# A two-layer decoder: a causal-attention batch stops counting as open from its first output product on

## The chip, the cores and the metric

The kernel runs on one core of one Trainium2 chip. The metric is the device time of one execution in microseconds (us), the median of several runs. Five engines work side by side: TensorE (in the profile PE for its matmuls and PEld for its weight loads), VectorE (DVE), ScalarE (ACT), GpSimd (POOL) and SyncE (SP), which here only issues data transfers (DMAs). Matmul results land in PSUM, in eight banks of 128 x 512 float32; everything else is held in SBUF.

## The reference

The input is four batches of 512 tokens by 512 features. Two layers follow, each with a self attention, a cross attention and a feed-forward part; after each of the six parts the result is added to its input and normalized over the features. The part that the change touches is the self attention of layer 1:

```python
kqv = x @ Wqkv + bqkv
kqv = kqv.reshape(b, s, 3, NUM_HEADS, HEAD_SIZE)        # 16 heads of 32
scores = jnp.einsum('bsnh,btnh->bnst', k, q) / math.sqrt(HEAD_SIZE)
scores = jnp.triu(scores) + -10000.0 * jnp.tril(ones, k=-1)
attn = jax.nn.softmax(scores, axis=2)
out = jnp.einsum('bnkq,bknh->bqnh', attn, v)
return out.reshape(b, s, NUM_HEADS * HEAD_SIZE) @ Wo + bo
...
x = _layernorm(x + _L1_attn_ref(x, L1_attn_Wqkv, L1_attn_bqkv, L1_attn_Wo, L1_attn_bo), axis=-1)
x = _layernorm(x + _L1_xattn_ref(x, ctx_2048, mask_BxS2_bk0), axis=-1)
x = _layernorm(x + _L1_ffn_ref(x, L1_ffn_gate_up_packed, L1_ffn_gate_up_scales, L1_ffn_down_packed, L1_ffn_down_scales), axis=-1)
```

The cross attention of layer 1 scores each token against its batch's 512 context rows, and the last feed-forward part works with 4-bit weights.

## The kernel before, in words

The six parts are called A to F, and a part with a batch is a task: D2 is the layer 1 self attention of batch 2, E0 the layer 1 cross attention of batch 0. Each task is a Python generator that emits instructions and yields at the end of a turn. `lanes` (line 1254) goes through the tasks in the order A0 to A3, B0 to B3, and so on to F3 (line 38). It keeps at most two tasks open; each round it lets every open task emit one turn, so the instructions of the two are interleaved. A new task opens when fewer than two are open, when the part before it is done for its batch, and when the task that was opened last has said `"next"` (lines 1263 to 1270). A task that has ended is taken off the list (lines 1273 to 1275).

The order in which turns are emitted isn't the order in which engines work. It is a priority: the compiler takes for each engine the earliest emitted instruction that is ready and finds a free tile, so a transfer or a transpose whose inputs are there can be moved far forward. Tiles come from shared pools: 69 of 2 KB a partition for operands (`op`), 13 for short-lived results (`tp`), 12 for the batches' x (`xp`, line 27), 4 for weights on their way, and the eight PSUM banks.

A self-attention task (`l1_attn`, line 820) loads its four x tiles, 128 tokens each, and then goes through these turns:

- three turns without work, then four with the 16 transposes of x (tile dx, line 828); its results are split into a high and a low half (dxh, dxl);
- the projections of the first four heads' keys and queries (dq, `project`, line 832) and the values (dv, line 872). A product of two such pairs is three matmuls (`mm3`, line 149). `stack` (line 848) copies the halves of each head into one tile (stk) by twelve DMAs a projection, on the queues of SP and POOL;
- 16 turns with one head each (line 961): scores (ds, line 908), maximum and mask on DVE (de, line 919), exponential on ACT (de, line 923), transposes (dT, line 933), copies (dpT, line 942), and for four heads at a time the product with the values (do, line 953). The further projections stand in the turns of heads 0, 1, 4, 5, 8 and 9. At head 7 (`D_NEXT`, line 968) the task says `"next"`;
- the drain of what is still queued, four transposes back to token order (dto, line 990), the merging with the sums of the masked part (line 981), four transposes to feature order (dF, line 996);
- four turns with the output products (dy, line 1007), each followed one turn later by the addition to x and its statistics (line 1001);
- the normalization (`finish`, line 229): four more turns, at whose end the x tiles are stored (line 238).

The bias of the output is added to x ahead of that, on POOL (line 994). Work that belongs to no batch is emitted beside certain tasks (`BESIDE`, line 40): beside D1 to D3 the 4-bit codes of the last part are unpacked on DVE (`l1_ffn_codes`, line 1061; lines 1074, 1075 and 1082), a block every third turn; beside E2 they are loaded back, with the rest of the last part's weights (`l1_ffn_weights`, line 1093).

The cross attention E (`l1_xattn`, line 1015) loads x, mask and context, transposes x (ex), computes scores (es, line 1048) and a softmax (lines 1041, 1042), transposes the weights (ep) and multiplies by the context (pv).

Of the kernel before, what the change touches and what calls it, by code (L numbers as in the profile page):

```python
# [68 lines left out]
class Net:  # L69
# [750 lines left out]
    def l1_attn(self, b):  # L820
# [183 lines left out]
        for i in range(NT):  # L1004
            pipe.tick()
            ps = self.pa("dy")
            self.mm3(ps, [(self.cols(oF[k], slice(i * P, (i + 1) * P)), self.w1[k, 3]) for k in range(NT)])
            pipe.later(1, add, ps, i)
            yield
        yield from pipe.drain()  # L1010
        self.finish(pipe, x, ln, 3, b)
        yield from pipe.drain()
# [241 lines left out]
def lanes(order, task, step):  # L1254

    todo = [(e.strip("+!"), e[0] == "+", max(1, e.count("!"))) for e in order]
    plain = [name for name, _, _ in todo]
    live, done = {}, set()  # L1260
    n, said = 0, 9
    while todo or live:
        if todo and len(live) < 2:
            name, soon, times = todo[0]
            before = chr(ord(name[0]) - 1) + name[1]
            if (before in done or before not in plain) and (said >= times or not live or soon):
                todo.pop(0)
                live[name] = task(name)
                last = name
                n, said = n + 1, 0  # L1270
        for name, g in list(live.items()):
            word = next(g, "end")
            if word == "end":
                live.pop(name)
                done.add(name)
            elif word == "next" and name == last:
                said += 1
        step(n)


def body(tc, args, phases=range(6)):
    with ExitStack() as ctx:
        net = Net(ctx, tc, args)
        net.gamma = net.load(net.c("gamma", [P, 1]), args["gamma"].to_broadcast([P, 1]))
        if 0 in phases:
            net.l0_attn_weights()
        net.bg = {("B", 0): net.l0_xattn_ctx(0), "C0": net.l0_ffn_scales(), "C": net.l0_ffn_weights(), "D": net.l1_attn_weights(), "F0": net.l1_ffn_codes(), "F": net.l1_ffn_weights()}
        f = [net.l0_attn, net.l0_xattn, net.l0_ffn, net.l1_attn, net.l1_xattn, net.l1_ffn]
        plain = ORDER.replace("+", "").replace("!", "").split()
        order = ORDER.split() if len(phases) == 6 else ["ABCDEF"[p] + str(b) for p in phases for b in range(B)]  # L1290

        def step(n):
            if len(phases) == 6:
                for first, last, key in BESIDE:
                    if plain.index(first) < n <= plain.index(last) + 1:
                        next(net.bg[key], None)

        def start(name):
            return f["ABCDEF".index(name[0])](int(name[1]))

        lanes(order, start, step)
# [68 lines left out]
```

## Time and profile before

| what | value |
|---|---|
| median of 3 runs | 1580.65 us |
| lowest and highest | 1579.52 and 1584.71 us |
| profiled execution, its own time | 1581.65 us |
| its span, first to last instruction | 1580.0 us |
| mean granted TensorE clock | 0.996 |
| PE busy | 1515.4 us |
| DVE, ACT, POOL busy | 1232.9, 1021.3, 666.2 us |

The profiled execution's time is 1.65 us above its span. Where things lie in it, by the views of the tiles: the transposes of x begin at 745.9 us for D0, 819.1 for D1, 941.2 for D2 and 1020.5 for D3; the first heads at 776.1, 859.3, 974.6 and 1061.5; the first output products at 903.4, 957.9, 1102.5 and 1158.1. The cross attention's transposes begin at 1141.2 (E0), 1181.7 (E1), 1194.7 (E2) and 1237.8 (E3). The first product of the last part (fg) begins around 1256 us.

A busy time is the union of an engine's instructions. A row of the view by stretches has the stretch, its length, and for each engine busy time and number of instructions, then the granted TensorE clock and the transfers' share and rate. A row of the order of time has start, length, engine, line, operation and tiles, and in brackets the engine's idle time before it with what ended it. A row of the waits has who waited, for whom, the total in us, how many times and the longest.

### The profile page before, as it was taken

Reading aid. Unit: us, or ns where it says so; the run is one execution under the profiler, and the core shown is the slowest. Engines: PE = TensorE matmul, PEld = TensorE weight load, DVE = VectorE, ACT = ScalarE, POOL = GpSimd, SP = SyncE. Lnnn points to the kernel's source line nnn. Section 1 sums busy time; section 2 is a strip of 40 time slices with the busy share of each in tenths; the row PEclk is TensorE's granted clock in tenths of the full one; section 3 lists DMA queues with packets and bytes.
Section 4 is the critical chain, followed back from the end, with each engine's and each line's share of the span. In section 5 each row is a group of like instructions: output and inputs, shape, how many; then the busy total and the mean of one; then the engine's idle time right before and its main releaser. Section 6 shows DMA issues by size and latency. Waiting matters only on the chain.

```text
span 1580.0 us, 25595 instructions
## 1 busy us (share of the span) xinstructions
PE 1515.4 (96%) x8222; PEld 1090.1 (69%) x8222; DVE 1232.9 (78%) x2658; ACT 1021.3 (65%) x2208; POOL 666.2 (42%) x672
## 2 busy tenths in 40 slices
PE   8999999999999999899999999999999999999996
PEld 6888786444544674477777668777687777777875
DVE  6486589999976688777577797767786888888896
ACT  5333336988878877888696864969634445545554
POOL 6673663555535303430435323353225344344342
PEclk9999999999999999999999999999999999999998
DMA  7043344455214744653434445633436630020101
GB/s 255 29 157 124 113 154 132 149 173 176 78 48 123 224 137 133 201 185 134 134 102 118 104 141 148 171 97 92 125 123 222 233 110 12 24 81 1 54 1 53
DMA packets 134150, 192.31 MB, mean 122 GB/s; under 512 B 17265, under 2 KB 52081, under 8 KB 134017
## 3 DMA queue, kind: packets, MB, share of 16 engines
q1 hardware_dynamic: 129888, 182.23, 36.3%
q0 software_dynamic: 4128, 8.46, 2.2%
q8 instruction: 65, 1.06, 0.3%
q14 instruction: 69, 0.56, 0.1%
HBM read 117.75 MB, written 47.71 MB: 105 GB/s over the span
## 4 chain that ended last, share of the span: by engine, by line
PE 63%; DVE 17%; ACT 8%; issue 6%; DMA 3%; POOL 3%; SPq 0%; ACTq 0%; DVEq 0%; POOLq 0%
PE fg L1185 7%; PE facc L1168 5%; PE dT L933 3%; DVE fg L1141 3%; PE pg L687 3%; PE had L755 2%; PE dn L741 2%; DVE bsm L474 2%; PE pu L689 2%; ACT de L923 2%; PE bo L498 2%; PE do L953 2%; PE qk L156 2%; PE qk L155 2%; PE qk L154 2%
## 5 line engine op out<-in xcount | busy, mean ns | idle before, releaser
L1141 DVE SCALAR_TENSOR_TENSOR fg<-fg,gs,fg 128x512 f32<-128x512 f32 x220 | 163.2, 745 | 30.9 <-ACT fg L1133 15.3
L923 ACT ACTIVATE de<-de,dm 128x128 f32<-128x128 f32 (+3 forms) x256 | 142.9, 563 | 11.3 <-DVE dm L919 10.9
L1185 PE MATMUL fg<-fxh,gu 128*128 128x512 f32 x352 | 140.2, 398 | 6.1 <-DVE fg L1141 3.1
L919 DVE CUSTOM_DVE_ANT_0 de<-ds,negm,thr 128x128 f32<-128x128 f32 (+3 forms) x256 | 126.4, 546 | 19.4 <-PE ds L908 16.0
L482 POOL TENSOR_SCALAR be<-be,bsm 128x512 f32<-128x512 f32 x128 | 96.5, 766 | 103.8 <-DVE bsm L480 72.7
L1185 PE MATMUL fg<-fxl,gu 128*128 128x512 f32 x352 | 137.4, 390 | 0.1
L664 POOL TENSOR_TENSOR hl<-g,hh 128x512 fp32r<-128x512 f32 x64 | 83.4, 1309 | 110.2 <-ACT hh L663 90.2
L1145 POOL TENSOR_TENSOR fg<-fg,fg 128x512 f32<-128x512 f32 x44 | 60.2, 1367 | 139.6 <-DVE fg L1141 60.0
L476 ACT ACTIVATE be<-bs,bsm 128x512 f32<-128x512 f32 x128 | 87.3, 690 | 31.1 <-DVE bsm L474 29.2
L845 POOL TENSOR_TENSOR dql<-dqf,dqh 128x512 fp32r<-128x512 f32 x32 | 41.4, 1295 | 150.8 <-ACT dqh L844 150.6
L933 PE MATMUL dT<-ident,de 128*128 128x128 f32 x640 | 92.0, 280 | 8.5 <-ACT de L923 6.4
L933 PEld LDWEIGHTS dT<-ident,de 128*128 128x128 f32 x640 | 72.3, 142 | 28.3 <-ACT de L923 14.0
L1185 PEld LDWEIGHTS fg<-fxh,gu 128*128 128x128 f32 x352 | 66.0, 188 | 30.1 <-DVE fg L1141 12.7
L474 DVE TENSOR_REDUCE bsm<-bs 128x1 f32<-128x512 f32 x128 | 83.4, 672 | 0.0
L498 PE MATMUL bo<-bpT,cT 128*64 128x512 f32 x256 | 76.7, 618 | 2.4 <-ACT bpT L489 1.2
L248 PEld LDWEIGHTS bT<-ident,be 128*128 128x128 f32 x512 | 54.9, 141 | 34.0 <-issue 11.5
L248 PE MATMUL bT<-ident,be 128*128 128x128 f32 x512 | 73.2, 281 | 3.6 <-POOL be L482 2.1
L1185 PEld LDWEIGHTS fg<-fxl,gu 128*128 128x128 f32 x352 | 66.1, 188 | 12.8 <-DVE fxl L146 0.4
L352 POOL TENSOR_TENSOR z<-z,rope_cos 128x512 f32<-128x512 f32 x32 | 46.8, 1473 | 64.8 <-DVE zs L349 57.8
L1133 ACT ACTIVATE fg<-fg,gs 128x512 f32<-128x512 f32 x88 | 60.1, 684 | 20.6 <-PE fg L1185 20.4
L687 PE MATMUL pg<-qT,tb 128*128 128x512 bf16 x256 | 66.8, 381 | 4.5 <-ACT qT L649 2.8
L1159 POOL TENSOR_TENSOR fhl<-fg,fhh 128x512 fp32r<-128x512 f32 x44 | 58.5, 1331 | 29.5 <-ACT fhh L1158 29.3
(355 smaller groups left out, 4640.3 us busy)
## 6 DMA issues: line engine op xcount, KB each, us to landing
x<-x SPq DMA_DIRECT2D x176, 256.0 KB, 3.0
had_scratch<-hw SPq DMA_DIRECT2D x64, 256.0 KB, 2.3
z<-had_scratch SPq DMA_DIRECT2D x64, 256.0 KB, 5.8
stk<-dqh SPq DMA_DIRECT2D x192, 64.0 KB, 2.1
tw<-in_wg_t SPq DMA_DIRECT2D x32, 256.0 KB, 3.8
tw<-in_wu_t SPq DMA_DIRECT2D x32, 256.0 KB, 3.7
tw<-in_wd_t SPq DMA_DIRECT2D x32, 256.0 KB, 2.8
p<-in_gu_p SPq DMA_DIRECT2D x22, 256.0 KB, 3.1
```

What stands on the lines that cost most here:

```text
L248: self.nc.tensor.transpose(pt[:, i * P : (i + 1) * P], srcs[i][:, j * P : (j + 1) * P], self.ident)
L474: nc.vector.tensor_reduce(sm[:, h : h + 1], ps, AX.X, ALU.max, negate=True)
L476: nc.scalar.activation(e, ps, AF.Exp, bias=sm[:, h : h + 1], accum_out=sm[:, 2 + h : 3 + h])
L482: nc.gpsimd.tensor_scalar(es[h][i], es[h][i], sm[:, 4 + h : 5 + h], 1.0, ALU.mult, ALU.mult)
L498: nc.tensor.matmul(po[0][h * 64 : h * 64 + 64, :], cT[j][:, c : c + 64], pTs[h], start=j == 0, stop=j == NT - 1)
L664: nc.gpsimd.tensor_tensor(lo, g, hi.bitcast(F32), ALU.subtract)
L687: nc.tensor.matmul(pg, tern["wg_t"][k, c][:, m], qT[k], start=k == 0, stop=k == NT - 1)
L919: nc.vector.tensor_tensor_reduce(es[i], ps, self.negm[:, 384 - P * i :], -1.0, self.thr[:, i : i + 1], ALU.add, ALU.min, n4[:, i : i + 1])
L923: nc.scalar.activation(es[i], es[i], AF.Exp, bias=n4[:, i : i + 1], scale=-1.0, accum_out=den[:, hh * 4 + i : hh * 4 + i + 1])
L933: nc.tensor.transpose(pt[:, o + (i - j) * P : o + (i - j + 1) * P], es[i][:, j * P : (j + 1) * P], self.ident)
L1141: self.emitted["DVE"] = nc.vector.scalar_tensor_tensor(y[u], ps, s, y[u], ALU.mult, ALU.add)
L1185: nc.tensor.matmul(ps, self.gu[i, u][:, g * P : (g + 1) * P], xT[g][n], start=n == 0, stop=n == 1)
```

## The change

At its first output product (i = 0) the attention task now yields the word `"tail"`. `lanes` notes the names that have said it, and no longer counts such a task among the open ones when it decides whether another may begin. The task itself goes on as before, one turn a round, until it ends. Only task D says `"tail"`; the other conditions for opening a task are the same. So while an attention batch is in its last nine turns, a third task may be open.

```diff
@@ -1006,7 +1006,7 @@
             ps = self.pa("dy")
             self.mm3(ps, [(self.cols(oF[k], slice(i * P, (i + 1) * P)), self.w1[k, 3]) for k in range(NT)])
             pipe.later(1, add, ps, i)
-            yield
+            yield "tail" if i == 0 else None
         yield from pipe.drain()
         self.finish(pipe, x, ln, 3, b)
         yield from pipe.drain()
@@ -1257,10 +1257,10 @@
 
     todo = [(e.strip("+!"), e[0] == "+", max(1, e.count("!"))) for e in order]
     plain = [name for name, _, _ in todo]
-    live, done = {}, set()
+    live, done, tails = {}, set(), set()
     n, said = 0, 9
     while todo or live:
-        if todo and len(live) < 2:
+        if todo and len(live.keys() - tails) < 2:
             name, soon, times = todo[0]
             before = chr(ord(name[0]) - 1) + name[1]
             if (before in done or before not in plain) and (said >= times or not live or soon):
@@ -1275,6 +1275,8 @@
                 done.add(name)
             elif word == "next" and name == last:
                 said += 1
+            elif word == "tail":
+                tails.add(name)
         step(n)
```

## The prediction

> **What bounds the kernel now.** I read four things in this order: the page, for the busiest engine; stretches of the span, for where that engine idles; the waits and the order of time in those stretches; and last the DMA queue, for whether loads are late.
>
> ```profile
> span 1580.0 us, 25595 instructions
> PE 1515.4 (96%) x8222; PEld 1090.1 (69%) x8222; DVE 1232.9 (78%) x2658; ACT 1021.3 (65%) x2208; POOL 666.2 (42%) x672
> ```
>
> TensorE (PE) is busy 96% of the span. The change doesn't alter a single piece of arithmetic, so it can only move PE's 64.6 us of idle time. Everything up to the first output product of attention batch D0 keeps its place; that product starts at 903.2 us (the view of the tile dy). So only idle time after 903 us is in play.
>
> Busy time by stretch; PE is the third number:
>
> ```profile
> core 0: us, PE busy (x) PEld busy (x) DVE busy (x) ACT busy (x) POOL busy (x), PEclk, DMA share, GB/s
> 850.00:900.00 50.00, 46.21 (x275) 35.75 (x273) 34.59 (x98) 36.91 (x98) 14.35 (x23) 1.00 0.46 125
> 900.00:950.00 50.00, 47.30 (x326) 34.15 (x325) 46.27 (x123) 32.33 (x92) 17.56 (x20) 1.00 0.42 133
> 950.00:1000.00 50.00, 49.89 (x252) 39.73 (x254) 37.41 (x97) 31.37 (x79) 16.91 (x26) 1.00 0.55 160
> 1050.00:1100.00 50.00, 48.62 (x289) 38.40 (x289) 34.65 (x99) 38.65 (x102) 17.10 (x26) 1.00 0.39 102
> 1100.00:1150.00 50.00, 47.03 (x317) 34.00 (x317) 38.82 (x106) 32.89 (x93) 16.79 (x20) 0.97 0.45 137
> 903.00:1180.00 277.00, 267.43 (x1665) 204.46 (x1664) 215.19 (x573) 186.10 (x501) 97.27 (x125) 0.99 0.43 125
> 1180.00:1260.00 80.00, 74.15 (x366) 58.29 (x364) 60.24 (x123) 38.12 (x83) 35.01 (x27) 1.00 0.69 240
> ```
>
> From 903 to 1180 us PE idles 277 - 267.43 = 9.6 us, and in the cross attention behind it (1180 to 1260) 80 - 74.15 = 5.9 us. All that this change could fill is therefore 15.5 us, 1% of the span. It isn't spread evenly: 2.70 us idle in 900:950 and 2.97 in 1100:1150, where D1 and D3 end their heads, but 0.11 in 950:1000, where D2 begins its heads with D1 nearly done.
>
> The order of time on PE at the end of D1's heads, and PE's waits from 903 to 1250 us (total, times, longest):
>
> ```profile
> 931.18 0.55 PE L933 MATMUL dT<-ident,de 128*128 128x128 f32 x3 [0.64 <-ACT de L923]
> 933.39 0.44 PE L933 MATMUL dT<-ident,de 128*128 128x128 f32 x2 [0.74 <-ACT de L923]
> 941.22 1.91 PE L248 MATMUL dx<-ident,x 128*128 128x128 f32 x16
> ```
>
> ```profile
> PE dT L933 <- ACT de L923: 4.7, 10, 0.7
> PE es L154 <- DVE exl L146: 1.5, 2, 1.3
> ```
>
> PE waits for ScalarE's exponentials, and D2's transposes (dx) stand ten microseconds behind these holes. Are they late because D2's input is late? The DMA queue says no:
>
> ```profile
> 769.10 2.02 SPq L238 DMA_DIRECT2D x<-x  x4
> 771.41 2.63 SPq L252 DMA_DIRECT2D x<-x  x4
> 1175.11 2.72 SPq L238 DMA_DIRECT2D x<-x  x4
> 1178.42 2.16 SPq L252 DMA_DIRECT2D x<-x  x4
> ```
>
> Each burst of four loads (L252) follows a burst of four stores (L238). The x pool has twelve tiles, three batches of four, so a load waits for the store of the batch three before it. D0's transposes began at 745.9 us, before the burst issued at 741.4 had all landed (747.2), so that burst was D1's and the one at 771.41 is D2's, behind C3's stores. D2's input was landed at 776.8 us, 164 us before its first transpose. The burst at 1178.42 is likewise E2's, behind D3's stores.
>
> **The change part by part.** No instruction is added or removed. By the generators, an attention batch takes 55 turns and its end is seen on the 56th: transposes on turns 4 to 7, first projections on 9 and 10, values on 11 to 14, heads on 15 to 30, output products on 47 to 50. Openings, counted from D0's: before D1 22, D2 56, D3 78, E0 112, E1 134, E2 143; after D1 22, D2 47, D3 69, E0 94, E1 116, E2 125. D2 comes 9 turns earlier, and E0 and all behind it 18. A turn saved isn't time saved: the PE work of the dropped turns stands in others.
>
> *Loads.* Four x loads per batch move forward on SP's queue. They have no value for D2, as shown. They are moved past D0's four stores; those wait for VectorE, not for SP, and the loads take 0.3 to 0.5 us each to issue. Zero; the cover is the 164 us.
>
> *The hole at the end of a batch's heads.* With D2's transposes (16, 1.91 us) and projections put before D1's drain, they can fill 2.70 us, and E0's can fill the 2.97 us beside D3. Bounds: 0 and -5.7. The third batch's own casts (dxh, 0.59 us each) join the ScalarE queue that PE is waiting for here, so I take half, -2.8. POOL's bias additions for D2 (four at L994) move from 942.9 into its gap from 906.7 to 935.0: nothing.
>
> By the Trainium skill (Perfetto Trace Analysis, Identifying the Most-Contended Engine) matmul occupancy is a poor measure of headroom and weight-load busy share is the better one. PE's weight loads are busy 11.39 us of 920:940 and 10.93 of 1120:1140 against a mean of 14.69 in twelve stretches of 20 us there; by that rule about 20 x 3.3/14.69 + 20 x 3.76/14.69, some 9.6 us, could be had, an estimate, and the sum would be 4 us below mine. I stay with the idle time, since this trace has the narrow value products (do) in just these stretches, whose loads take 0.11 us each against the usual 0.19.
>
> *The start of D2's heads.* Before, D2's heads start at 974.6 us beside the last of D1, idle 0.11. After, the distance D1 to D2 is 25 turns, so they start beside D1's merges and output transposes, just as D1's heads stood beside D0's (22 turns; 850:900, idle 3.79) and D3's beside D2's (1050:1100, idle 1.38). Bounds: +1.3 and +3.7; I take the mean of the two, (3.79 + 1.38)/2 - 0.11 = +2.5.
>
> *E2's input.* This is a new wait. E2 opened 10 turns after D3's end; now it is 1 turn. Its x tiles are D3's. From D3's last output product (1169.2) through add, statistics, normalization, store and load to E2's landed tiles (1184.7) took 15.5 us. Work that PE surely has behind that product is E1's 16 transposes at 0.11 and 48 score products at 0.227, 12.6 us. What is left is 2.9 us. Queued behind the load on SP are E1's and E2's context loads. Bounds: 0 (the compiler's order finds other PE work, such as E0's last products) and 15.5 (none is left over). I take +2.9.
>
> *Background steps.* The code unpacking beside D1 to D3 needs some 70 turns and had 90; it now gets 72. It ends about where E0 opens and stays covered by heads: zero. Uncovered, the rest would be pumped where the last layer first asks for it: per block 0.65 + 0.52 + 0.55 us of VectorE, so two blocks left over cost 3.4 us.
>
> Sum: -2.8 + 2.5 + 2.9 = +2.6 us. The profiled execution took 1581.65 us, 1.65 more than its span and 1.0 above the median 1580.65. Against the median this makes 1583.2.
>
> **The rivals.**
>
> *A, the forecast: holes move.* Two are half filled and two open. Own range -2 to +8 us.
>
> *B, the third batch really fills.* PE takes D2's and E0's work in every hole, and D2's head start finds D3's projections as cover. For it: 950:1000 shows that PE can run at 99.8% with this mixture of work, and ScalarE has room (32.33 of 50). Against it: the trace also has 46.21 of 50 in a stretch with two open batches. Half of the 15.5 us goes, 8 us: 1572.6.
>
> *C, slower: the 69 shared tiles.* The attention's weights and bias hold 33, which leaves 36, and one batch alone needs up to 36 of them around its seventh head (counted over its turns in the code). Head stacks (stk) already wait on SP for tiles that other heads still read:
>
> ```profile
> SPq L853 <- ACT dpT L942: 19.5, 7, 7.6
> SPq L853 <- PE do L953: 12.2, 4, 10.8
> ```
>
> PE hardly notices today: D0's second stack landed at 790.6 us and head 4 began at 792.6, 2.0 us later. It decides once a stack is more than these 2 us later than now. With D1, D2 and D3 crowded alike, one longest wait of 7.6 less 2.0 at each of three later stacks of D2 is 16.8 us; 1581.65 + 16.8 - 1.0 = 1597.4. Against it: the pair D0 and D1 has the same crowding at 22 turns and lost only 3.79 us in its worst stretch. The Trainium skill (Perfetto Trace Analysis, Optimization Strategy) says that a recurring gap on the engine that should be saturated can mean too little buffer space for the next tile; that speaks against a third batch on unchanged pools, and it would make the sum that of this rival.
>
> *D, nothing moves.* The compiler already hoists what is ready (D2's loads), so an earlier place would leave the same order: 1580.65. Against it: D2's transposes were ready for 164 us and weren't hoisted.
>
> **How the numbers follow.** A 0.50 (0.02 faster, 0.28 same, 0.20 slower, as its range reaches past the bound of 4.7 us mostly upwards), B 0.27 (0.25 faster, 0.02 same), C 0.19, all slower, D 0.04, same. That gives faster 0.27, same 0.34, slower 0.39; 0.3% is about what a measurement of this kernel tells from no change. For the range, B's far end is 15.5 us below and C's price 16.8 above; leaving about one in ten on either side I take 1568 to 1600, and for A alone 1578 to 1589.
>
> **What would show it.** In the trace after: D2's dx before D1's last dT, at about 925 us, and no 0.7 us holes for de there (first term); idle over 1.3 us in the 50 us around D2's first heads (second); PE idle between E1's last score product and E2's transposes, ended by E2's x (third); x load bursts of D2 unmoved at 771. I am wrong towards B if D1's and D2's heads keep below 1 us idle in 50, and towards C if PE's ds waits for stk.

## The result, and the profile after

The median went from 1582.18 us (four runs of the kernel before beside it) to 1594.88 (1594.06 to 1595.62): 12.7 us slower, a ratio of 1.0076 with a 95% interval of 1.0063 to 1.0089. The forecast, 1583.2, had the sign and a fifth of the size. The wide range held the result, the likeliest case's own range (-2 to +8) did not.

The page's first lines and, from the view by stretches, the rows that answer to those of before (behind the stretch and its length stands PE's busy time; the granted clock stands ahead of the transfers' share and rate; the third answers to 1100:1150 before, as D3 is 11.6 us later by then):

```profile
span 1593.7 us, 25591 instructions
PE 1520.5 (95%) x8222; PEld 1095.0 (69%) x8222; DVE 1230.6 (77%) x2658; ACT 1022.3 (64%) x2208; POOL 662.7 (42%) x672
```

```profile
core 0: us, PE busy (x) PEld busy (x) DVE busy (x) ACT busy (x) POOL busy (x), PEclk, DMA share, GB/s
900.00:950.00 50.00, 48.62 (x329) 35.59 (x329) 42.79 (x114) 35.79 (x98) 19.91 (x24) 1.00 0.40 126
950.00:1000.00 50.00, 43.33 (x208) 33.59 (x210) 26.13 (x71) 27.99 (x70) 11.51 (x18) 0.90 0.35 93
1111.60:1161.60 50.00, 46.41 (x305) 33.41 (x304) 35.76 (x102) 35.87 (x100) 20.04 (x24) 0.97 0.45 137
821.20:1581.10 759.90, 728.66 (x3847) 569.57 (x3845) 596.31 (x1302) 453.98 (x1042) 286.94 (x287) 0.99 0.33 99
```

The last row is a measure that the rest of this section uses: **the stretch** from D1's first dx to TensorE's last instruction, which holds the same 3847 matmuls in every kernel that was compared. Before, it reads:

```profile
819.10:1567.50 748.40, 722.83 (x3847) 564.48 (x3845) 599.95 (x1302) 452.99 (x1043) 289.02 (x287) 1.00 0.33 100
```

So the change costs 11.5 us there, in two halves: idle time rose from 748.40 - 722.83 = 25.57 us to 759.90 - 728.66 = 31.24, +5.7, and the same matmuls took 5.8 us longer, mostly because the granted clock was lower for a time (by rows of 5 us, busy time times the missing share of the clock makes 6.7 us after and 1.5 before). The stretch is the steadier measure of a mechanism: by D0's first dx, before anything had changed, the profiled executions of these kernels already stood 4.5 us earlier to 5.8 us later than the one of before. But it is one execution of each kernel, so the medians give the verdicts.

Nearly all of it is lost in one place. D2's dx came 11.3 us earlier than before (929.9 for 941.2) and D2's first head 7.7 us earlier; by D3's first head (1073.1 for 1061.5) the kernel was 11.6 us late, from 2.0 us late at D1's first head, which is outside the change's reach. The order of time on PE there (start, length, tile, and in brackets the idle time before it and what ended it):

```profile
929.94 0.60 PE L248 MATMUL dx<-ident,x 128*128 128x128 f32 x4
...
966.61 0.50 PE L894 MATMUL suf<-dvh,after 128*128 128x512 f32 x1 [2.56 <-ACT dvh L862]
...
986.70 0.51 PE L908 MATMUL ds<-stk,stk 96*128 96x256 f32 x2 [0.56 <-ACT dqf L840]
...
988.26 0.45 PE L908 MATMUL ds<-stk,stk 96*128 96x384 f32 x1 [1.06 <-DVE dm L919]
989.43 0.79 PE L908 MATMUL ds<-stk,stk 96*128 96x512 f32 x1 [0.72 <-DVE dm L919]
991.18 1.12 PE L248 MATMUL dF<-ident,do 128*128 128x128 f32 x4 [0.96 <-DVE dm L919]
```

Two holes are new: one of 2.56 us at 964.0, where the first sum of the masked part (suf) waits for the high half of a value tile (dvh), and a row of four, 3.3 us together, from 986 to 991, where PE and VectorE wait for each other by turns: PE for a bank that VectorE has just read (dm), VectorE, idle for 0.64 and 1.00 us, for the next score product. It looks as if one bank at a time were free. PE's waits from 900 to 1250 us name both, and a third at D3's end (do); none of these was there before with more than 0.2 us:

```profile
PE ds L908 <- DVE dm L919: 2.6, 6, 1.1
PE suf L894 <- ACT dvh L862: 2.6, 1, 2.6
PE do L953 <- DVE exl L146: 1.6, 1, 1.6
```

Behind each of the two the clock falls. Before, all rows of 900 to 1000 us had 1.00:

```profile
960.00:965.00 5.00, 4.04 (x18) 3.00 (x16) 3.34 (x6) 0.89 (x2) 0.00 (x0) 1.00 0.38 141
965.00:970.00 5.00, 3.39 (x12) 2.86 (x13) 3.42 (x10) 3.13 (x9) 3.19 (x5) 0.80 0.41 92
970.00:975.00 5.00, 5.00 (x28) 4.28 (x27) 2.44 (x9) 2.55 (x7) 0.65 (x1) 0.86 0.43 121
...
990.00:995.00 5.00, 4.04 (x15) 3.33 (x15) 2.05 (x4) 3.70 (x10) 0.00 (x0) 0.50 0.00 0
```

In the slow rows a matmul of the projections takes 0.63 us instead of 0.39.

The first hole is read from ScalarE's order of time. After:

```profile
964.08 0.69 ACT L840 ACTIVATE dqf<-dq,b 128x512 f32<-128x512 f32 x1 [4.20 <-PE dq L156]
964.80 0.62 ACT L844 CAST dqh<-dqf 128x512 fp32r<-128x512 f32 x1
965.32 0.58 ACT L861 COPY dv<-dv 128x512 f32<-128x512 f32 x1
965.93 0.62 ACT L862 CAST dvh<-dv 128x512 fp32r<-128x512 f32 x1
```

And before:

```profile
968.93 0.59 ACT L861 COPY dv<-dv 128x512 f32<-128x512 f32 x1 [4.20 <-PE dv L156]
969.55 0.62 ACT L862 CAST dvh<-dv 128x512 fp32r<-128x512 f32 x1
974.37 0.69 ACT L840 ACTIVATE dqf<-dq,b 128x512 f32<-128x512 f32 x1 [4.20 <-PE dq L156]
```

The order on ScalarE is swapped. D2's fourth value tile left PE at 961.3 us, but ScalarE, idle for 4.20 us in all, waited for the projection dq, which its order has first; only then came the copy and the cast that suf needs. Before, the copies stood first, and D1's output products and that same projection gave PE some 5 us of work between the value (968.9 us) and the sum (974.2). After the change D1's output products come at 1003 us, behind all this: D1's merge is late too.

### The profile page after: what moved, and what is told of

It reads as the page before. It is cut to its first block, busy times and chain, and to the rows that moved or that the text cites. A ratio compares the mean times of both kernels' runs of the same rounds, so it can differ in the third digit from the quotient of the medians.

```text
span 1593.7 us, 25591 instructions
## 1 busy us (share of the span) xinstructions
PE 1520.5 (95%) x8222; PEld 1095.0 (69%) x8222; DVE 1230.6 (77%) x2658; ACT 1022.3 (64%) x2208; POOL 662.7 (42%) x672
## 4 chain that ended last, share of the span: by engine, by line
PE 60%; DVE 18%; ACT 8%; issue 6%; DMA 4%; POOL 3%; SPq 1%; ACTq 0%; DVEq 0%; POOLq 0%
PE fg L1185 7%; PE facc L1168 5%; PE dT L933 3%; DVE fg L1141 3%; PE pg L687 2%; DVE bsm L474 2%; PE pu L689 2%; PE dn L741 2%; PE bo L498 2%; ACT de L923 2%; PE do L953 2%; PE had L755 2%; PE bT L248 2%; DVE x L235 2%; PE dq L154 2%
## 5 line engine op out<-in xcount | busy, mean ns | idle before, releaser
L248 PEld LDWEIGHTS bT<-ident,be 128*128 128x128 f32 x512 | 55.0, 141 | 33.8 <-issue 11.5
```

Of the source, the lines that this page charges most:

```text
L248: self.nc.tensor.transpose(pt[:, i * P : (i + 1) * P], srcs[i][:, j * P : (j + 1) * P], self.ident)
```

## The experiments

Four experiments came first. They ask which batch's early start costs, and whether the swap or the crowd of three batches is the cause. Times given as "+" are medians against the kernel before as it ran beside them (1579.83 us here).

**Only D2 early.** D1's and D2's tails go on counting.

```diff
-            yield "tail" if i == 0 else None
+            yield "tail" if i == 0 and b == 0 else None
```

> Only D0 says tail, so D2 opens 9 turns earlier and E0 is not brought forward by D2's tail. Crowding theory (the loss is made where D2's values and heads stand beside D1's merges, output transposes and output products, about 960 to 1035 us of the profile after): most of the loss stays, +8 to +11 us against before. Rival (the loss is made at the other end, where E0 opens beside D3's last heads): at most +3 us.

Measured: 1607.17 us, +27.3, ratio 1.0168 (1.0150 to 1.0187): both expectations missed, this is twice the loss of the whole change. D3 opens only when D1 has ended, so D2 and D3 stand further apart than in either kernel, and D3 meets the same swap, alone against D2's tail:

```profile
1085.94 0.80 PE L894 MATMUL suf<-dvh,after 128*128 128x512 f32 x1 [3.43 <-ACT dvh L862]
```

The run has the two holes of the changed kernel at D2, and then its own at D3. It shows that D2's early start is no gain that the later ones spoil. That the distance between two batches acts through what it puts beside a batch's first sum is how I read the hole at D3.

**Only E0 early.** The same edit with `b == 2`.

> Only D2 says tail: D0 to D3 stay as before, E0 opens 9 turns earlier. Crowding theory: 0 to +3 us against before. Rival (E0's opening costs): +8 us or more. The two kernels e1 and e2 should add up to about the loss of the change, +12 us, if nothing else plays in.

Measured: 1584.22 us, +4.4, ratio 1.0024 (1.0013 to 1.0034), 3.5 us in the stretch (751.9 for 748.4). This lies between its two expectations, and the two runs don't add up to the change, though that was expected of them: 27.3 and 4.4 us for 12.7. By the medians E0's early start by itself is a loss, a third of the whole. One place of it is the end of D3's heads: VectorE's rows there are, in this run,

```profile
1134.10 3.82 DVE L235 TENSOR_SCALAR x<-x,ln 128x512 f32<-128x512 f32 x4
1137.84 0.41 DVE L1030 TENSOR_SCALAR pen<-mk 128x512 f32<-128x512 uint8 x1
1138.18 0.68 DVE L146 TENSOR_TENSOR exl<-ex,exh 128x512 fp32r<-128x512 f32 x1
1138.78 0.67 DVE L942 COPY dpT<-dT 128x512 f32<-128x512 f32 x1
```

and in the kernel before

```profile
1132.18 1.91 DVE L235 TENSOR_SCALAR x<-x,ln 128x512 f32<-128x512 f32 x4
```

D2's normalization of four tiles takes twice as long, and E0's mask and split stand ahead of the copy dpT that D3's value product needs. PE idles 0.68, 0.64 and 1.58 us there. The same row of 3.81 us, and a hole of 1.59, are in the changed kernel at 1144.68 and 1147.89. But over the whole stretch PE's idle time is only 0.9 us longer here (751.90 - 725.44 = 26.46 for 25.57); the other 2.6 us are busy time, at a lower clock. About 1.5 of them lie at D1's end (930 to 940 us), ahead of E0, behind holes of 0.64, 0.16 and 0.74 us that the kernel before has there to the hundredth. This run's row and that of before:

```profile
935.00:940.00 5.00, 5.00 (x27) 2.20 (x30) 3.21 (x4) 1.17 (x2) 4.82 (x6) 0.77 0.80 276
935.00:940.00 5.00, 5.00 (x43) 2.29 (x42) 4.06 (x5) 1.32 (x3) 5.00 (x6) 1.00 0.80 277
```

**The order on ScalarE mended.** The changed kernel, with the second projection's first copy issued behind the fourth value's cast.

```diff
-                nc.scalar.activation(f, ps, AF.Identity, bias=self.b1[:, 12 + m : 13 + m], scale=32.0 ** -0.5)
+                with self.tc.issue_after(self.v_done.ins) if m == 1 else nullcontext():
+                    nc.scalar.activation(f, ps, AF.Identity, bias=self.b1[:, 12 + m : 13 + m], scale=32.0 ** -0.5)
...
-            nc.scalar.copy(hi, f)
+            self.v_done = nc.scalar.copy(hi, f)
```

> The change, and the first half of the fourth query and key projection (dqf) may be issued on ScalarE only behind the casts of the fourth value tile. In the profile after, ScalarE had these the other way round for D2, and PE stood 2.56 us until the value cast was done; the clock granted in the next 10 us was 0.80 and 0.86. Theory that this order makes the hole: it closes, 3 to 5 us are gained against the change (about +8 against before). Rival (the value tile could not have been copied earlier, its target tiles were taken): the hole stays, +12 against before.

Measured: 1587.66 us, +7.8, ratio 1.0046 (1.0029 to 1.0062). The stretch fell from 759.9 to 755.1. The hole of 2.56 us is gone, and the loss with it is about twice the hole: 4.8 us, of which 2.9 is idle time (31.24 to 28.3) and 1.8 PE's busy time (728.66 to 726.84). Here the clock that fell behind the hole added almost two thirds to its price.

**D2's heads held back.** The changed kernel with nine empty turns of D2 between its values and its heads.

```diff
+        for _ in range(9 if b == 2 else 0):
+            pipe.tick()
+            yield
```

> The change, and D2 makes nine empty turns behind its values: its transposes, first projections and values are early, its heads start at the same turn as before the change, and D3 opens at the same turn as before. Crowding theory with the heads as its cause: the loss is gone, -3 to +3 us against before. If the early values and projections alone make it: +6 us or more.

Measured: 1589.70 us, +9.9, ratio 1.0056 (1.0040 to 1.0071), 756.7 us in the stretch. This fits the second expectation; E0's early start is still in it. With D2's heads held back, most of the loss stays. It has moved: now D1's merge is cut up, by an unpacking step that VectorE's order has ahead of the multiplication (line 987 here, 984 otherwise) and whose codes arrive late.

```profile
959.20 0.55 DVE L1077 TENSOR_SCALAR p<-p,i 128x512 int32<-128x512 int32 x1 [3.37 <-DMA p<-in_gu_p]
959.66 0.69 DVE L987 TENSOR_TENSOR do<-do,dm 128x512 f32<-128x512 f32 x1
```

```profile
960.40 0.66 PE L248 MATMUL dF<-ident,do 128*128 128x128 f32 x4 [0.83 <-DVE do L987]
962.60 0.69 PE L248 MATMUL dF<-ident,do 128*128 128x128 f32 x4 [1.54 <-DVE do L987]
964.73 1.11 PE L248 MATMUL dF<-ident,do 128*128 128x128 f32 x4 [1.45 <-DVE do L987]
```

What remained open was whether a shortage of tiles makes the second row of holes, and of which. Four more runs, beside 1581.31 us of before.

**Only D2's dx early.** The nine empty turns stand before D2's first projection instead.

> The changed kernel, with nine empty turns of D2 behind its transposed input and before its first projection: D2's loads and its dx still come beside D1's last heads, its projections, values and heads go back to where they stood before. If the loss is made by D2's projections and values taking operand tiles and ScalarE time beside D1's merges, most of it goes: what is left is what the run with the tail for D2 alone showed (E0 early, +4.4 us), less the hole of about 1.3 us that dx fills at D1's end: +2 to +5 us against the kernel before. If it is made by D1's last steps being spread over more time whenever a third batch takes turns at all, the loss stays at +8 us or more.

Measured: 1587.76 us, +6.5, ratio 1.0044 (1.0032 to 1.0056): between the two expectations. The stretch, 752.1, is within 0.2 us of that of the run with E0 alone, and D3's first head is only 0.3 us later relative to D1's; the rest of the median's 6.5 was lost ahead of the stretch (its profiled execution was 4.7 us late at D0's first dx), where nothing differs from the kernel before in what is computed. I read it as the first expectation, with that reserve: D2's projections, values and heads make the loss at D2, not its loads and dx. The dx gained nothing either, as a hole of 2.24 us opened behind D1's merge (dF behind DVE's do).

**One more short-lived tile.**

```diff
-O_BUFS, T_BUFS, X_BUFS, W_BUFS = 69, 13, 12, 4
+O_BUFS, T_BUFS, X_BUFS, W_BUFS = 69, 14, 12, 4
...
-        gs = self.load(self.c("gs16", [P, 88], F16), a["gu_s"])
+        gs = self.load(self.w("gs16", F16)[:, :88], a["gu_s"])
```

> The changed kernel with 14 instead of 13 tiles in the pool of dqf, dqh, dql, de and e (room made by giving the 88 columns of layer 2's small table a tile that is there anyway). If the idle time of TensorE between D2's first score products (ds, behind DVE's de, which waited for a dqh tile) is a shortage of this pool, it goes, with the slow clock after it: 3 to 6 us less than the changed kernel, +7 to +10 against before. If the shortage is of the matmul banks, or only the order on ScalarE counts, nothing moves: within 2 us of the changed kernel (+13).

Measured: 1590.58 us, +9.3, ratio 1.0058 (1.0045 to 1.0071), which is in the range of the first expectation; but the stretch took 759.9 us, the same as the changed kernel to the tenth, and this execution had been 4.5 us early before it. I follow the trace, which speaks for the second expectation: the first hole is there, and the row of holes behind it,

```profile
982.24 0.41 PE L908 MATMUL ds<-stk,stk 96*128 96x384 f32 x1 [0.95 <-DVE dm L919]
983.38 0.51 PE L908 MATMUL ds<-stk,stk 96*128 96x512 f32 x1 [0.72 <-DVE dm L919]
```

The tile that VectorE seemed to wait for, one of this pool, is not what is short.

**One more operand tile, in the changed kernel and in the kernel before.** As above, with 70 and 13.

> The changed kernel with 70 instead of 69 shared operand tiles (room made as in the run with 14 tiles). If three batches at once run short of these tiles, one more gives back 4 to 8 us: +5 to +9 against before, and more than the same tile gives the kernel before. If the loss is one of order alone, it stays within 2 us of the changed kernel (+13).

> The kernel before with 70 instead of 69 shared operand tiles. If the shortage is the changed kernel's own, the kernel before gains nothing: 0 us, within 2. If it is there in both, the kernel before gains 3 to 6 us as well.

Measured: the changed kernel came to 1588.17 us, +6.9, ratio 1.0037 (1.0022 to 1.0052), and its stretch to 753.3, 6.6 us less; the kernel before came to 1583.95 us, +2.6, ratio 1.0015 (1.0004 to 1.0026), its stretch to 749.2. The first is as expected, the second outside both of its ranges. In the changed kernel the second row of holes is gone; the first, 2.56 us, is still there, since the swap on ScalarE is. PE's idle time in the stretch is 753.30 - 728.62 = 24.7 us, less than before the change.

But not all of these 6.6 us lie where three batches are open. In the 50 us around D1's first heads, beside D0, where the change has done nothing yet, PE idled 3.79 us in 850:900 of the kernel before. With 70 tiles it idles 1.52 us there in both kernels; this is the kernel before with 70:

```profile
853.60:903.60 50.00, 48.48 (x284) 37.74 (x283) 35.60 (x102) 38.65 (x103) 15.66 (x24) 1.00 0.43 125
```

With 14 short-lived tiles nothing is gained there, so it is the operand tile. The 69 tiles are therefore short for two batches too, and 2.3 of the 6.6 us are a gain that the kernel before has as well. Its stretch is no shorter for it, as its matmuls took 2.7 us longer (725.49 for 722.83); why the clock was lower in that execution isn't shown.

Which tile is short for three batches can be read from ScalarE. From 930 to 982 us it has the same instructions in the same order in the changed kernel with 69 and with 70 tiles. Then the one with 70 (first line) copies two results of the transposes in a row, dT to dpT, where the one with 69 copies one and the next only 8 us later:

```profile
983.95 1.05 ACT L942 COPY dpT<-dT 128x512 f32<-128x512 f32 x2
982.10 0.57 ACT L942 COPY dpT<-dT 128x512 f32<-128x512 f32 x1
990.26 0.59 ACT L942 COPY dpT<-dT 128x512 f32<-128x512 f32 x1
```

dpT is an operand tile, and until it is copied a dT keeps its bank. The late copy starts 0.04 us behind the end of the row's last score product (989.43 + 0.79), which is the last reader of two stacks from the same pool; in the other five kernels with 69 tiles and such a row this distance is 0.04 to 0.09 us. So I read a ring: dpT waits for a tile that a stack holds, the stack for its score products, and these for a bank that a dT holds. No view names a wait for a free tile, so the ring is a reading of these six kernels.

The last four ask whether the parts add up, beside 1580.11 us of before.

**Both cures.** Order mended and 70 tiles.

> The changed kernel with both cures at once: ScalarE's order mended (the fourth value tile's copies ahead of the second projection's) and 70 operand tiles. The stretch read is that from D1's first dx to TensorE's last instruction, 748.3 us before and 11.6 us more with the change. The order alone left +6.7 in it, the tile alone +4.9. If they are two separate losses (a hole of 2.56 us and what the slow clock adds to it, and the later wait for tiles), both together leave what E0's early start costs: +2 to +4 us in the stretch and in the time. If both cure the same loss, nothing is added: +5 to +7.

Measured: 1582.28 us, +2.2, ratio 1.0012 (1.0001 to 1.0022). The stretch, by its row:

```profile
824.50:1572.60 748.10, 725.67 (x3847) 565.12 (x3845) 598.72 (x1302) 453.00 (x1043) 286.51 (x287) 1.00 0.32 100
```

The time is as the first expectation has it, the stretch lies below it. Two separate losses, then: 4.8 us for the order and 6.6 for the tile make 11.4, and both together take 11.8 away. It is plainer in the 50 us around D2's first heads (950:1000 after the change, with 6.67 us idle). With the order mended, with 70 tiles, and with both:

```profile
947.80:997.80 50.00, 45.89 (x245) 35.63 (x244) 30.92 (x86) 31.94 (x84) 15.33 (x25) 0.93 0.37 101
954.90:1004.90 50.00, 45.89 (x255) 35.58 (x254) 32.94 (x93) 32.44 (x88) 14.21 (x23) 0.97 0.40 108
954.50:1004.50 50.00, 48.44 (x278) 37.93 (x277) 37.54 (x103) 35.48 (x96) 14.04 (x23) 1.00 0.43 119
```

Each cure takes 2.56 us of idle time away, and both take 5.11. The stretch is at the value of before although E0 is still early; what pays for that is the tile's 2.3 us at D1's first heads, which the change has no part in.

**Both cures, and E0 not early.** As the last, with the word only for D0 and D1.

```diff
-            yield "tail" if i == 0 else None
+            yield "tail" if i == 0 and b < 2 else None
```

> As the run before it in this list, and E0 is not let in early: only the batches D0 and D1 stop counting at their first output product. If the loss has these three parts and no fourth, the time comes back to that of the kernel before: -2 to +2 us, the bottom end if D2's dx in the hole at D1's end is worth anything. If a third batch beside D1's tail costs something by itself, +3 us or more stays.

Measured: 1579.21 us, -0.9, ratio 0.9997 (0.9989 to 1.0006): no difference from the kernel before. That is the expectation for three parts and no fourth. The stretch:

```profile
819.60:1564.80 745.20, 722.53 (x3847) 564.21 (x3845) 602.35 (x1302) 452.55 (x1043) 288.27 (x287) 1.00 0.32 101
```

It is 3.2 us shorter than before, 2.9 of it idle time. Of these, 2.3 are again the tile's at D1's first heads. What the early D2 itself moves cancels: at D1's end PE idles 1.17 us instead of 2.70, around D2's first heads 1.66 instead of 0.11. So that the early D2 and D3 are worth anything isn't shown. Nor does a fourth loss hide behind the tile's gain: beside the kernel before with 70 tiles, PE's idle time in the stretch is 1.0 us less (22.67 for 23.71).

**Only E0's part taken out.** The last edit in the changed kernel, without the cures.

> The changed kernel, only without E0's early start (D2's tail does not count). If E0's part is separate, it takes 3 to 4 us off the change's loss: +7 to +10 us against before, +8 in the stretch from D1's first dx to the end. If E0's early start has already hidden in the other losses, +11 or more stays.

Measured: 1588.15 us, +8.0, ratio 1.0049 (1.0037 to 1.0061); 758.3 us in the stretch. The time is as the first expectation has it, the stretch, 9.9 us above before, is not. By the medians E0's part is 12.7 - 8.0 = 4.7 us, by the stretches 1.6; by the two runs ahead of this one, with and without E0 early, it is 3.1 (medians) and 2.9 (stretches). So it is separate, and its size lies between 1.6 and 4.7 us.

**The word three turns later.** `i == 3` in place of `i == 0`.

> The changed kernel with the word three turns later, at the last output product instead of the first, so that the next batch opens some three turns (about 7 us) later, at most two turns ahead of where it opened before. If the loss follows how far D2's projections and values reach into D1's merges, it falls to below half: 0 to +6 us against before. If it hangs on details of the order (which copy stands first on ScalarE), it can be anything between -3 and +14 and follows no dose: a hole of over 2 us ahead of D2's first suf tells it.

Measured: 1598.44 us, +18.3, ratio 1.0110 (1.0095 to 1.0124), 765.8 us in the stretch: outside both ranges, though the sign that was named for the second, a hole of over 2 us, is there. A smaller dose of the change costs more than the whole. The marks of both losses are there: the swap,

```profile
965.85 0.79 PE L894 MATMUL suf<-dvh,after 128*128 128x512 f32 x1 [2.29 <-ACT dvh L862]
...
968.75 0.80 PE L894 MATMUL suf<-dvl,after 128*128 128x512 f32 x1 [0.94 <-DVE dvl L863]
```

and the row of waits of ds on VectorE twice, from 988.9 to 993.7 and from 1003.2 to 1008.1 us. The loss follows no dose; it hangs on which instruction stands first in an order, and on whether the pool of operand tiles runs out.

## Why the prediction was right or wrong

- **Loads, zero: right.** D2's x loads stand at 773.50 us, 2.1 us later than before like all else there, and D2's dx was not held by them.
- **The hole at the end of a batch's heads, -2.8: half right in the changed kernel.** D2's dx stands beside D1's last heads as forecast, and 900:950 idles 1.38 us instead of 2.70. But D3's end got worse, 3.59 us idle in 1111.6:1161.6 where 1100:1150 had 2.97. The step assumed that E0's transposes would fill that hole; E0's splits on VectorE, and D2's normalization, slowed beside E0's subtractions on GpSimd, made a new one (the run with E0 alone). In the kernel with the losses taken out the gain at D1's end is there too, 1.5 us. The other reckoning, by weight loads, put the sum 4 us lower by holding its 9.6 us against the uncut 5.7; cut in half like these, it is 2 us lower, and nothing of that size came.
- **The start of D2's heads, +2.5: the step that failed, by its size.** It took the mean of two stretches in which heads of two batches stood together, 1.38 and 3.79 us idle, and held 3.7 for the upper bound. Measured were 6.67 us idle in 950:1000 against 0.11, and some 4 us more of slow clock around these holes. The model stretches had three conditions that the new place lacked. ScalarE's order was right in them: D1's, D3's and, before, D2's value copies stood ahead of the next projection. Their operand tiles served two batches, not three, and were short even so, as 2.3 of the 3.79 us go with one tile more. And an idle time was taken at its own length, while here the clock fell behind it: of the 4.8 us of the first hole only 2.9 were idle time. With both cures the same 50 us idle 1.56 us, 1.45 more than before, which is within the step's bounds of 1.3 and 3.7: it priced the crowding, and not the swap and the tile.
- **E2's input, +2.9: wrong, zero.** E2's four loads went out at 1196.66 us, right behind the four stores of 1194.28 and ahead of D3's stores at 1201.17; its transposes came at 1207.4. By VectorE's normalizations just ahead (four tiles from 1193.71, four from 1200.60, the latter behind D3's last output product of 1194.7) the first stores are E0's: E2 took tiles that came free earlier than D3's. The step assumed D3's tiles from the order of opening, and that order no longer held.

```profile
773.50 2.64 SPq L252 DMA_DIRECT2D x<-x  x4
1194.28 2.29 SPq L238 DMA_DIRECT2D x<-x  x4
1196.66 2.10 SPq L252 DMA_DIRECT2D x<-x  x4
1201.17 2.04 SPq L238 DMA_DIRECT2D x<-x  x4
```

- **Background steps, zero: right for their end, wrong as a cover.** Nothing was left over behind E0 (from E1's first transposes to the end the two kernels stay within 0.9 us of each other). But the step looked at the number of turns alone. In the run with D2's heads held back an unpacking step in VectorE's order waited 3.37 us for its codes, with D1's merge behind it.
- **Rival B, the third batch fills: no.** Its reason, that PE could run at 99.8% with this mixture in 950:1000, was read from a place whose work the change took away: D1's output products, 957.9 us before and 1003.0 after.
- **Rival C, the shared tiles: right in the cause, wrong in the way.** The change does run short of operand tiles, and one more gives it 6.6 us of stretch, 2.3 of which the kernel before saves in idle time as well. But C's sign, PE's ds waiting for stk, never came. SP's copies did wait up to 17.1 us in 940 to 1010, where 4.5 was their longest before, but no wait of PE ends with one of them; by the reading above the tile that was late is dpT, and it held up ds through the banks. C counted the pair D0 and D1, with 3.79 us in its worst stretch, against itself; most of that was a shortage of these tiles. C's price, 16.8 us, came from stk's waits and is near the 12.7 for another reason than its own.

```profile
SPq L853 <- PE do L953: 17.1, 1, 17.1
```

In the sum: the gain at D1's end was there, the third term wasn't, and the second was about four times too small (2.5 us for 6.6 of idle time and some 4 of slow clock). That the range held the result is luck: it is owed to C, whose weight was 0.19 and whose price had another reason.

Open are three things: why the clock falls behind some holes and not behind others of the same length; why the word for D0 alone and the word three turns later cost more than the change, beyond the holes that their profiles show; and whether the kernel with all cures is faster at all.

## What to carry to other kernels

Letting a third task in moves no work by itself: it changes the order in which each engine gets its instructions and the number of tiles in use. Before forecasting a gain, read the idle time that it could fill, and then, at the new neighbours' first waits, whose copy stands first on the engine with an order of its own and how many tiles the pools have left. Where an early start loses, mend order and buffers one at a time and then together: the sum tells whether these were the causes. Here two small cures and one withheld word turned 12.7 us into none. And read a cure where it acts, and in the kernel before as well: 2.3 us of the tile's gain lay in a place that the change never touched, and the totals alone would have credited them to the change.

## What was not expected of the hardware

**Short holes can lower the clock.** The granted clock was 0.80 and 0.86 in the two rows behind a single hole of 2.56 us, 0.57 and 0.74 in the run with the word three turns later, behind 2.29 and 0.94 us, and 0.50 behind 3.3 us of holes spread over five. The Trainium skill (TensorE: Matmul & The Clock Gate, HAM oscillation) gives as its rule that idle gaps should stay under some 3.4 us. Here shorter ones were enough at times, and half of the change's loss in the stretch, 5.8 of 11.5 us, is slow matmuls. But the length of a hole alone doesn't decide it in these runs: behind the 2.24 us of the run with only D2's dx early the clock stayed at 1.00, and the holes of 0.64, 0.16 and 0.74 us at D1's end left it at 1.00 in the kernel before and at 0.77 in the run with E0 alone.

**VectorE beside GpSimd.** The four instructions of a normalization took 1.91 us together with GpSimd idle for most of it, and 3.81 with two subtractions of GpSimd (ecTl) beside them; those took 1.44 us each, where one at 1140.80, with no normalization beside it, took 1.27:

```profile
1144.88 2.87 POOL L146 TENSOR_TENSOR ecTl<-ecT,ecTh 128x512 fp32r<-128x512 f32 x2 [2.81 <-ACT ecTh L143]
```

In this row both engines pay, and VectorE pays double. The Trainium skill (Advanced Engine Details and Errata, VectorE Performance Modes) says that the second VectorE port to SBUF is shared with GpSimd and that the two hinder each other in the modes that use it; this row agrees with it.
